# A decoder layer on one core: another order of attention's pools in SBUF

## The chip, the cores and the metric

The kernel runs on one core of a Trainium2 chip. The metric is the device time in microseconds of one execution. A core has five engines that run side by side, each strictly in its own order: TensorE (PE, matrix products; PEld is its loading of weights), VectorE (DVE), ScalarE (ACT), GpSimd (POOL) and SyncE (SP). SP only issues transfers (DMAs); ACT and POOL issue some as well. Engines wait for each other, and for the landing of transfers, by semaphores. SBUF is the working memory on the chip, PSUM the small memory in which TensorE leaves its products, HBM the large memory outside.

## The reference

The input x has 16 sequences of 112 rows of 1024 numbers, 1792 rows in all; ctx has 375 rows for each sequence.

```python
x = _layernorm(x + _L0_attn_ref(x, w_gate, w_up, w_down), axis=-1)      # "x1" in this text
x = _layernorm(x + _L0_xattn_ref(x, ctx, ctx, Wq, Wk, Wv, Wo), axis=-1)
x = _layernorm(x + _L0_ffn_ref(x, qweight, qscale, qzeros), axis=-1)
```

The first step, in spite of its name, is a gated MLP: silu(x w_gate^T), with the half of each row that is smallest in magnitude set to zero, times x w_up^T, times w_down^T. The second is attention of x1 over ctx:

```python
q = (query @ Wq).reshape(b, sq, NUM_HEADS, HEAD_DIM).transpose(0, 2, 1, 3)   # 32 heads of 32
k = (key @ Wk).reshape(b, sk, NUM_KV_HEADS, HEAD_DIM).transpose(0, 2, 1, 3)  # 8, each repeated 4 times
v = (value @ Wv).reshape(b, sk, NUM_KV_HEADS, HEAD_DIM).transpose(0, 2, 1, 3)
probs = jax.nn.softmax(jnp.einsum('bhqd,bhkd->bhqk', q, k) * scale, axis=-1)
out = jnp.einsum('bhqk,bhkd->bhqd', probs, v)
return out.transpose(0, 2, 1, 3).reshape(b, sq, DIM) @ Wo
```

The third is a product with a weight matrix that is stored as 4-bit numbers with scales and zeros.

## The kernel before

The work is done in stages. First come the gates, with the search for each row's median, the up projection, and the keys and values of attention, which are stored to HBM as k_d and v_d. Then comes the down projection in several passes (class Down). Its last pass, `last_pass`, goes over seven pairs of row tiles of 128 rows. For each tile it adds up the products in a tile y (L853 loads the rows of x into it, L859, L874, L875 and L882 add to it), takes the layer norm in place (L72 to L87) and has POOL store it to HBM as 128 rows of x1, `x1_d` (L863). The names in a trace leave numbers out, so this store reads `x_d<-y`. The last of the fourteen stores is the last thing that the MLP does. Beside it, the last pass unpacks the 4-bit weights (L912 to L921) and loads the weights of the query projection, wq_sb. Queries are made for two sequences at a time, from x1 as it is read back from HBM: `fetch` loads 112 rows (xr, L939), `rows` transposes them on TensorE (L950) and ACT copies them out (L951), and `chunk` makes one of eight blocks of 128 query columns (L958, L962). Of the first pair of sequences the first block is made before attention begins.

Then `attention_and_ffn` runs. Its loop goes over 128 units n. A unit is a sequence b, a half c of the key heads (0 or 1) and a number r of four, so four units in a row share one tile of keys, kT_b_c. A unit makes the scores of four heads (L1025), their maxima on DVE (L1031), and their exponentials on ACT into one of three slots of the tile probs (L1033). One unit later the exponentials are divided by their sums (L1041 on DVE, L1042 on POOL), two units later DVE transposes them in blocks of 32 by 32 into a tile named squares (L1053). After every second unit sixteen DMAs move the blocks of the two units to their places in a tile named weights (L1067): eleven are issued by SP, five by POOL. Some units later TensorE multiplies these with the values (L1080), and when a row tile is complete it is projected with wo_sb (L1117) and taken through the last two layer norms (class Tail). Between a unit's scores and those of the next, TensorE makes a chunk of queries or a piece of a projection; two chunks follow unit 0.

Before the loop SP gets, in this order, the keys kT_0_0 (L1004), the two value tiles of sequence 0 (L1008), and wo_sb, the whole matrix Wo of 4 MB, in sixteen DMAs of 256 KB (L1246). The next keys, kT_0_1, which unit 4 is the first to use, are asked for in unit 1, so they come behind wo_sb in SP's order. The first DVE instruction of attention is the memset of the padding of probs (L999).

The order of instructions on each engine is the order in which the program is written (`as_written`). What a framework adds are addresses and semaphores. SBUF is given out by pools. On the left side they are stacked: a pool that is opened later stands at a higher address. When a pool is opened on space that earlier tiles had, its first instructions wait until every earlier instruction on that space is done, and for a DMA that reads or writes there until it has landed. In `attention_and_ffn` five such pools are opened: const (wo_sb), ld (keys, values, rows of x1), work (probs, squares, weights, results), small (sums, maxima, statistics), and the pools in PSUM. The last pass keeps its y tiles on the right side, in a pool that is closed when attention begins.

DMAs that SP and ACT issue carry one of eight semaphores each in turn; a DMA waits until the earlier one with its semaphore has landed. The DMAs that POOL issues have eight of their own.

The bytes of a partition at which these tiles stand, from the built program:

| tile | before |
|---|---|
| parts of the down weights (wd), in use to the end of the last pass | 17312 to 62368 |
| blocks h of the last pass | 62368 to 84896 |
| sums c11, u, v | 84896 to 127904 |
| statistics of the last pass | 132320 to 132548 |
| y, four buffers | 132576 to 148960 |
| wo_sb | 17312 to 50080 |
| keys, values, rows of x1 (ld) | 50080 to 68448 |
| probs, squares, weights and the rest of work | 68448 to 152416 |
| sums, maxima and statistics (small) | 152416 to 153124 |

Of the kernel before, what the change touches and what calls it, by code (L numbers as in the profile page):

```python
# [10 lines left out]
F32 = mybir.dt.float32  # L11
# [11 lines left out]
P = 128  # L23
B, S, D = 16, 112, 1024
NT = B * S
TT = NT // P
KC = D // P
# [937 lines left out]
def attention_and_ffn(nc, tc, ident, ident_b, negh, x1_d, k_d, v_d, queries, wf_sb, wo, out):  # L965
# [14 lines left out]


    with ExitStack() as ctx:
        const = ctx.enter_context(tc.tile_pool(name="a_const", bufs=1))
        wo_sb = const.tile([P, KC, D], F32, tag="wo", name="wo_sb")

        ld = ctx.enter_context(tc.tile_pool(name="a_ld", bufs=2))
        work = ctx.enter_context(tc.tile_pool(name="a_work", bufs=2))
        small = ctx.enter_context(tc.tile_pool(name="a_small", bufs=3))
        ps = ctx.enter_context(tc.tile_pool(name="ps", bufs=3, space=PSUM))
        ps_s = ctx.enter_context(tc.tile_pool(name="ps_s", bufs=1, space=PSUM))  # L990
        ps_o = ctx.enter_context(tc.tile_pool(name="ps_o", bufs=1, space=PSUM))
# [371 lines left out]
def kernel(  # L1363
# [38 lines left out]
    with as_written(nc, tc):  # L1402
        with ExitStack() as psum:
# [30 lines left out]
            for mc in range(EARLY):  # L1434
                queries.chunk(0, mc)
        attention_and_ffn(nc, tc, ident, ident_b, negh, x1_d, k_d, v_d, queries, wf_sb, wo, out)


# [46 lines left out]
```

## Time and profile before

| what | us |
|---|---|
| median of three runs | 2598.56 (2598.23 to 2599.01) |
| the profiled execution | 2598.46 |
| its span, from its first to its last instruction | 2596.7 |
| TensorE busy in the span | 2517.4 (97%) |
| DVE, ACT, POOL busy | 1719.4, 1390.3, 1205.1 |
| mean granted clock of TensorE | 0.987 |
| last store of x1 issued by POOL | 1844.40 |
| wo_sb: first and last of its sixteen loads issued by SP | 1839.1, 1863.2 |
| first product that reads wo_sb | 1961.1 |

The span holds everything that the profile shows; some 1.8 us of the execution lie around it. The MLP takes the first 1840 us, attention with the third step the rest. TensorE is busy nearly all the time in both, so the places to look at are those where it is not, and what ended its idle time there. A line of a timeline gives start, length, engine, line, operation, tiles and count, and in brackets the engine's idle time before it with what ended it. A line of the chain of waits gives start, length, and the engine and line (or the transfer) that the end of the program goes back to at that time. For a DMA the issue is on the queue of its engine (SPq, POOLq, ACTq), and the landing is a time of its own.

### The profile page before, as it was taken

The page shows a single profiled execution, that of the slowest core. Times are in us where ns is not written, and L with a number is a line of the kernel's source. Part 1 is how long each engine was busy: PE and PEld are TensorE (multiplying, and loading weights), DVE is VectorE, ACT ScalarE, POOL GpSimd, SP SyncE. Part 2 cuts the span into 40 slices and gives each one's busy share as a digit, 9 for nine tenths or more (in the row PEclk, how much of TensorE's full clock was granted, in tenths as well). Part 3 has the DMA queues.
Part 4 walks back from the last instruction along what each step waited for, and adds up shares of the span by engine and source line. Part 5 has one row for each costly group of instructions (what it writes and reads, how often), then busy time and mean ns, then how long its engine had stood idle before and what let it go on. Part 6 is the DMA issues. An engine that isn't in the chain of part 4 may idle for free. (4 is left out here: it accounts for less than half of the span.)

```text
span 2596.7 us, 34788 instructions
## 1 busy us (share of the span) xinstructions
PE 2517.4 (97%) x10500; PEld 1526.5 (59%) x10514; DVE 1719.4 (66%) x3634; ACT 1390.3 (54%) x2470; POOL 1205.1 (46%) x1143
## 2 busy tenths in 40 slices
PE   9999999999999999999988999999889999999996
PEld 4444444466666666777764444444566666666763
DVE  0378778878988887677730343247577777777773
ACT  0487787778767877888830000000255565555652
POOL 1113443255557545444250000024387888878883
PEclk9999999999999999999999999999889999999998
DMA  6322322276768668998657223157587778787763
GB/s 243 132 72 83 109 107 73 99 273 237 228 228 281 229 229 275 299 291 290 224 172 251 87 87 109 55 189 232 147 205 186 204 191 199 192 200 197 196 175 95
DMA packets 283609, 478.65 MB, mean 184 GB/s; under 512 B 37856, under 2 KB 208224, under 8 KB 279328
## 3 DMA queue, kind: packets, MB, share of 16 engines
q1 hardware_dynamic: 241184, 374.06, 46.9%
q0 software_dynamic: 27008, 75.76, 9.4%
q10 hardware_dynamic: 15232, 26.62, 3.3%
q8 instruction: 85, 1.39, 0.2%
q14 instruction: 100, 0.82, 0.1%
HBM read 272.12 MB, written 103.50 MB: 145 GB/s over the span
## 5 line engine op out<-in xcount | busy, mean ns | idle before, releaser
L468 ACT ACTIVATE ja<-a,cand 128x1824 int8<-128x1824 f32 x434 | 787.9, 1815 | 195.2 <-DVE cand L480 187.3
L471 DVE TENSOR_SCALAR_CACHE_REDUCE jv<-a,cand 128x928 uint8<-128x928 f32 x434 | 509.6, 1174 | 42.6 <-ACT a L455 35.7
L190 PE MATMUL pg<-wg_sb,xT 128*128 128x456 f32 (+1 forms) x1344 | 519.2, 550 | 2.7 <-DMA wg_sb<-in_wg_dram 2.7
L190 PEld LDWEIGHTS pg<-wg_sb,xT 128*128 128x128 f32 x1344 | 255.8, 191 | 265.6 <-issue 258.7
L1033 ACT ACTIVATE probs<-sc,nmax 128x375 f32<-128x375 f32 x512 | 286.3, 572 | 229.7 <-DVE nmax L1031 213.0
L1042 POOL TENSOR_TENSOR probs<-probs,sums 128x1500 f32<-128x1500 f32 x128 | 344.2, 2689 | 131.8 <-DVE sums L1041 112.8
L1031 DVE TENSOR_REDUCE nmax<-sc 128x2 f32<-128x750 f32 x256 | 228.4, 931 | 128.4 <-PE sc L1025 128.2
L729 PE MATMUL m<-wd,h 128*128 128x512 f32 (+1 forms) x616 | 267.1, 596 | 6.1 <-DMA h<-hT_d 6.1
L297 PE MATMUL pu<-u,xe 128*128 128x344 f32 x896 | 264.1, 453 | 2.3 <-DVE u L317 1.8
L1053 DVE STREAM_TRANSPOSE squares<-probs 128x1536 f32<-128x1536 f32 x128 | 224.0, 1750 | 20.3 <-DMA weights<-squares 10.4
L297 PEld LDWEIGHTS pu<-u,xe 128*128 128x128 f32 x896 | 170.0, 190 | 92.4 <-DVE u L317 2.9
L201 POOL DMA_DIRECT2D s_d<-s x84 | 45.9, 546 | 360.7 <-DVE s L200 297.3
L958 PE MATMUL bank<-x1T,wq_sb 128*128 128x224 f32 x1008 | 210.4, 363 | 0.0
L958 PEld LDWEIGHTS bank<-x1T,wq_sb 128*128 128x128 f32 x1008 | 188.3, 192 | 34.5 <-issue 31.3
L729 PEld LDWEIGHTS m<-wd,h 128*128 128x128 f32 (+1 forms) x616 | 117.5, 191 | 153.8 <-issue 152.3
L297 PE MATMUL pu<-u,xl 128*128 128x344 f32 x672 | 199.6, 453 | 2.5 <-DVE c L330 1.4
L1117 PE MATMUL bank<-wo_sb,aT 128*128 128x256 f32 x832 | 194.6, 388 | 0.0
L951 ACT COPY x1T<-pq 128x448 f32<-128x448 f32 x4 | 1.9, 535 | 349.1 <-DMA sc<-in_qs_dram 331.8
L1117 PEld LDWEIGHTS bank<-wo_sb,aT 128*128 128x128 f32 x832 | 155.1, 191 | 45.9 <-issue 23.3
L1067 POOL DMA_DIRECT2D weights<-squares x320 | 177.7, 561 | 6.9 <-PE po L1080 2.4
L375 PE MATMUL pk<-wv_sb,ctx 128*128 128x256 f32 (+1 forms) x768 | 173.3, 379 | 0.0
L421 POOL TENSOR_TENSOR hs<-hs,hm 128x512 f32<-128x512 f32 (+1 forms) x84 | 96.7, 1159 | 160.8 <-DMA hm<-m_d 151.5
(152 smaller groups left out, 3372.6 us busy)
## 6 DMA issues: line engine op xcount, KB each, us to landing
weights<-squares SPq DMA_DIRECT2D x704, 96.0 KB, 3.4
h<-hT_d SPq DMA_DIRECT2D x56, 640.0 KB, 4.6
weights<-squares POOLq DMA_DIRECT2D x320, 96.0 KB, 3.6
ctx<-in_ctxT_dram SPq DMA_DIRECT2D x16, 1500.0 KB, 8.8
a<-s_d SPq DMA_DIRECT2D x14, 1376.0 KB, 8.5
us<-s_d SPq DMA_DIRECT2D x112, 172.0 KB, 3.7
u_d<-c SPq DMA_DIRECT2D x84, 172.0 KB, 3.2
xe<-in_xT_dram SPq DMA_DIRECT2D x28, 512.0 KB, 5.5
```

Of the source, the lines that this page charges most:

```text
L190: nc.tensor.matmul(pg[:, :w], xts[t][:, kc, :], wg_sb[:, kc, ds(off, w)], start=(kc == 0), stop=(kc == KC - 1),)
L297: nc.tensor.matmul(m, a[i][:, b, ts(n, P)], k[:, n, :], start=(n == 0), stop=(n == KH - 1))
L468: nc.scalar.activation(ja, a[:, NV:], AF.Sign, bias=cand, scale=-1.0, accum_out=st["sgn"])
L471: nc.vector.tensor_scalar(jv, a[:, :NV], cand, -(TOPK - 1 - NA / 2), ALU.is_lt, ALU.add, accum_out=st["nlt"])
L729: self.nc.tensor.matmul(bank, a[:r, k, :], b(k)[:r], start=(k == 0), stop=(k == HK - 1),)
L958: nc.tensor.matmul(pq[:, :GT], self.wq_sb[:, kc, ts(mc, P)], self.x1T[g][:, kc, :], start=(kc == 0), stop=(kc == KC - 1),)
L1031: nc.vector.tensor_reduce(nmax[h], sc[h][:, :, :SK], AX.X, ALU.max, negate=True)
L1033: nc.scalar.activation(pr[:, i, :SK], sc[i // 2][:, i % 2, :SK], AF.Exp, bias=nmax[i // 2][:, i % 2 : i % 2 + 1], accum_out=sums[:, i : i ...
L1042: nc.gpsimd.tensor_tensor(pr, pr, sums.unsqueeze(2).to_broadcast([P, 4, SK]), ALU.mult)
L1053: nc.vector.transpose(sq[:, :, n % 2].rearrange("p k (i f) -> p k i f", f=Q), probs[:, n % 3].rearrange("p i (k f) -> p k i f", f=Q),)
L1067: queue.dma_start(wt[ts(m, Q), :, j], by_part[ts(j, Q), :, m])
L1117: nc.tensor.matmul(pp[:, :256], aT[:, h, r, :], wo_sb[:, h * REP + r, ts(i, 256)], start=(h == 0 and r == 0), stop=(h == 1 and r == REP - 1),)
```

## The change

Two lines go from the top of `attention_and_ffn`'s list of pools to a place behind its pools on the left side.

```diff
     with ExitStack() as ctx:
-        const = ctx.enter_context(tc.tile_pool(name="a_const", bufs=1))
-        wo_sb = const.tile([P, KC, D], F32, tag="wo", name="wo_sb")
 
         ld = ctx.enter_context(tc.tile_pool(name="a_ld", bufs=2))
         work = ctx.enter_context(tc.tile_pool(name="a_work", bufs=2))
         small = ctx.enter_context(tc.tile_pool(name="a_small", bufs=3))
+        const = ctx.enter_context(tc.tile_pool(name="a_const", bufs=1))
+        wo_sb = const.tile([P, KC, D], F32, tag="wo", name="wo_sb")
         ps = ctx.enter_context(tc.tile_pool(name="ps", bufs=3, space=PSUM))
```

The addresses that follow from it, with what stood there in the last pass:

| tile | after | stands where |
|---|---|---|
| keys, values, rows of x1 (ld) | 17312 to 35680 | wd was |
| probs | 35680 to 54112 | wd was |
| squares, weights and the rest of work | 54112 to 119648 | wd, h, c11, u and part of v were |
| sums, maxima and statistics (small) | 119648 to 120384 | v was |
| wo_sb | 120384 to 153152 | the rest of v, the statistics, y, and tiles of the unpacking were |

The two built programs have the same instructions in the same order on every engine; what differs in them are addresses and the semaphores that some instructions wait for. In the program of before, the memset (L999) waits for the landing of the last four stores of x1, and the first of the sixteen loads of wo_sb waits for none of them. In the changed program the memset waits for nothing, and the first load of wo_sb waits for these four stores and for DVE's last layer norm.

## The prediction

> **What bounds the kernel now.** I read the busy shares first, then the stretches around the one place that the change touches, then the waits, the chain and the queues there.
>
> ```profile
> PE 2517.4 (97%) x10500; PEld 1526.5 (59%) x10514; DVE 1719.4 (66%) x3634; ACT 1390.3 (54%) x2470; POOL 1205.1 (46%) x1143
> ...
> 1843.00:1860.00 17.00, 6.52 (x36) 6.13 (x38) 2.65 (x4) 4.10 (x11) 0.85 (x2) 0.74 0.82 200
> 1860.00:1886.00 26.00, 26.00 (x160) 19.86 (x152) 17.40 (x21) 14.60 (x48) 17.92 (x14) 0.91 0.60 139
> ```
>
> The columns of a stretch are its length, then PE, weight loads, DVE, ACT and POOL busy, granted clock, DMA share and GB/s. TensorE is full nearly everywhere; where attention begins it works 6.52 of 17 us. So what is worth anything here is TensorE time between the last product of the MLP and attention's steady run. Who makes it wait:
>
> ```profile
> 1842.64 6.32 PE L958 MATMUL bank<-x1T,wq_sb 128*128 128x224 f32 x32
> 1859.44 1.63 PE L1025 MATMUL sc<-kT,qT 32*128 32x375 f32 x8 [10.48 <-ACT qT L962]
> ...
> 1843.29 0.81 DVE L87 TENSOR_SCALAR y<-y,ln_mv,ln_rstd 128x1024 f32<-128x1024 f32 x1 [0.69 <-POOL ln_rstd L82]
> 1854.47 0.15 DVE L999 MEMSET probs<- 128x108 f32 x1 [10.36 <-DMA x_d<-y]
> ```
>
> TensorE's 10.48 is DVE's 10.36 passed on: the memset of probs (L999) stands until the last rows of x1 have landed, and behind it in DVE's order stand the maxima of unit 0 (L1031), then ACT's exponentials, then the freed banks that unit 1's scores want. The chain shows the same stretch and what follows:
>
> ```profile
> 1844.40 9.89 DMA x_d<-y
> ...
> 1859.44 1.63 PE sc L1025 x8
> 1861.07 5.12 PE bank L958 x16
> 1866.19 0.84 PE sc L1025 x8
> 1867.03 3.22 PE bank L958 x16
> 1870.26 1.06 PE sc L1025 x8
> 1871.32 3.22 PE bank L958 x16
> 1874.54 0.90 PE sc L1025 x8
> ```
>
> After the gap the same work is slow: 1.63 against 0.84 for the scores of a unit, 5.12 against 3.22 for a chunk of queries, 2.69 us together (the granted clock of the stretch from 1860 is 0.91). The piece at 1874.54 is unit 4, the first to use the second key tile, kT_0_1. That tile is loaded by SP, which works in order:
>
> ```profile
> 1837.47 1.60 SPq L1008 DMA_DIRECT2D v<-v_d  x2
> 1839.11 24.71 SPq L1246 DMA_DIRECT2D wo_sb<-in_wo_dram  x16
> 1863.87 0.58 SPq L1004 DMA_DIRECT2D kT<-k_d  x1
> 1874.73 7.12 SPq L1067 DMA_DIRECT2D weights<-squares  x11
> ...
> SPq L1246 <- DMA xr<-x_d: 12.0, 1, 12.0
> ```
>
> The 24.71 us hold a stall of 12.0: eleven of the sixteen loads go out by 1848.1, the twelfth at 1860.7, since it shares a semaphore with the fetch of xr (L939), which ACT issues only at 1856.85, behind its own wait for DVE.
>
> **The change part by part.** No instruction is added, removed or moved: the instruction lists of the two built programs have the same rows in the same order on PE, DVE, ACT and SP, and on POOL but for which copies carry a wait. Only addresses move, and with them waits.
>
> (1) Wait taken away. The memset, the exponential table load and the first weights copy lose their waits for the stores of x1. The memset waits for nothing then. DVE is free at 1843.29 + 0.81 = 1844.10, so the memset goes 10.37 us earlier, unit 0's maxima too (its scores are done at 1841.80 + 0.91 = 1842.71), and unit 1's scores at 1859.44 - 10.36 = 1849.08. TensorE's two query chunks end at 1842.64 + 6.32 = 1848.96, so they cover all but 0.1 us, the gap is gone, and with it the slow 2.69. From unit 1 the warm steps are 0.84 + 3.23 (from 1866.19 to 1870.26, 4.07) and 4.28 (to 1874.54); I take 4.10 + 4.07 + 4.28 = 12.45. TensorE stands before unit 4 at 1861.5 instead of 1874.54: 13.0 us early. DVE and ACT keep step, having done units 2 and 3 at that pace.
>
> (2) Wait added. The first load of wo_sb now waits for those stores, on SP, and behind it stand fifteen more loads, kT_0_1, and the eleven weights copies of units 0 and 1. When does kT_0_1 land?
> - The last store is issued at 1844.40. It took 9.89 because the loads of wo_sb were in the queues; the two before it, at 1827.77 and 1836.30, took 3.0 and 3.3. With 3.3 it lands at 1847.7 (ends 3.0 and 4.0, the latter its longest time beside other loads: -0.3, +0.7).
> - The stall of 12.0 is over: xr is issued 10.3 earlier, 1846.5, and lands 3.9 later, before the twelfth load needs it.
> - wo_sb: the load issued at 1860.71 into empty queues took 3.98, the next landed 1.69 after it, the next three 1.28, 1.30 and 1.30 apart (256 KB each). In the earlier burst the first took 5.2 and nine landings were 1.29 apart. So 1847.75 + 3.98 + 1.69 + 14 x 1.29 = 1871.5 for the sixteenth. Low end, by the mean of all ten intervals of the first burst, 1.21: -1.7; high end +1.2 for a first load of 5.2.
> - kT_0_1 was issued 0.64 after the last load of wo_sb and landed 0.24 after it, 6.63 in all, though a key tile alone takes 3.1 (the one at 1837.08). So it lands behind all of wo_sb: 1871.7.
>
> TensorE waits for it from 1861.5 to 1871.7, 10.2 us, with nothing in its order to cover it: queries and scores are queued strictly. A gap as long as the old one leaves it slow for the same two pieces: 2.69 again (ends 0 and 6.8, half of the 13.65 us for which the clock record at this place shows a half).
>
> (3) The queue behind. The weights copies of units 0 and 1 follow on SP once their semaphores come round, the last at about 1874 and landed by 1877; the product that reads them (L1080) comes after unit 6's scores, in before 1884.50 - 1874.54 = 9.96 after unit 4 started, so now past 1881: at least 4 us of cover. Without it each us late would be paid. wo_sb itself is read first at 1961.1, 89 us after landing. xr comes earlier, for transposes at 1882.79 in before.
>
> (4) Traffic beside wo_sb. Five copies by POOL (480 KB) and xr (448 KB) now run while wo_sb comes in. Bounds: nothing, since beside the x1 store the landings of wo_sb stayed 1.29 apart; or their bytes at wo_sb's own 256 KB per 1.29, 928 / 256 x 1.29 = 4.7 us. The row for a transfer beside wo_sb is the former, so I take 0 and keep 4.7.
>
> The Trainium skill, page "DMA: Bandwidth & Descriptors", section "Queues, rings and completion order", speaks against the change here: each DMA engine takes turns, packet by packet, between the queues that have work, so POOL's copies and xr would push the loads back. By it the 4.7 would count and the sum would be 4.6 slower. The same page, section "Where 436 GB/s comes from", puts the HBM limit of a core near 358 GB/s, 0.73 us per load; by it (an estimate) wo_sb would be in by 1863.6 and the sum about 11 us faster. The landings 1.29 apart contradict that rate for these loads, and the measurement decides.
>
> **Sum.** -13.0 + 10.2 + 2.69 = -0.1 us: unit 4 has lost what unit 1 gained. Against the span of 2596.7 that is 2596.6. The profiled run took 2598.46, 1.8 over its span, and the median of three is 2598.56, so it stands for them; I forecast 2598.5. Its own range, with the ends (-0.3 -1.7 -2.7 and +0.7 +1.2 +4.7), is 2594 to 2605.
>
> **The rivals.**
> A, faster: kT_0_1 does not sit behind all of wo_sb, or wo_sb runs faster without the store between. Issued when the ninth load has landed (1847.75 + 3.98 + 1.69 + 7 x 1.29 = 1862.5) and taking 3.1, it lands at 1865.6; TensorE waits 4.1, slow for 0 to 2.69. -13.0 + 4.1 + 1.3 = -7.6: 2591.0; with no wait at all, -13.0: 2585.6. For it: 404 GB/s moved in the best slice near 1851. Against it: 6.63 for kT_0_1 where nothing but wo_sb was ahead.
> B, slower: the copies by POOL and xr hold the loads up by the 4.7 of part 4, so kT_0_1 lands at 1876.4: 2603.2. It costs from the moment that kT_0_1 lands after 1871.8, and passes 0.2% when it lands after 1877. For it: copies of 96 KB took 2.3 alone and up to 6.2 in company around 1890. Against it: the unchanged landings beside the store.
> C: the change does not do what it says, and the memset still waits: 2598.6. Only the trace can show a semaphore that comes late, but the built program gives the memset none.
>
> **How the numbers follow.** Forecast 0.66, A 0.18, B 0.14, C 0.02. About 0.2% (5.2 us) is what a measurement of this kernel can tell from no change. Faster by more: A, and a little of the forecast's lower edge, 0.20. Slower by more: half of B, and edges, 0.12. Within: 0.68. The range reaches down to A's middle and up past B: 2591.5 to 2604.
>
> **What would show it.** Part 1: the memset beside L87 with no idle time, unit 1's scores near 1849 at 0.84, no gap there. Part 2: SP's wo_sb starting near 1847.7, the store of 1844.40 landing in some 3 us, the loads in one run with no stall of 12, kT_0_1 issued about 1862.5 and landing near 1871.7, and a gap of some 10 us on TensorE before unit 4, with 1.63 and 5.12 after it. Part 3: no wait of the products at L1080 near 1884. I am wrong if that gap is under 5 us (A), if it ends after 1877 (B), or if the stretch from 1886 to 1947, where TensorE idled 1.1 and 5.6 us in before, changes by several us for another reason.

## The result and the profile after

The changed kernel took 2607.24 us, the median of 13 runs (2600.26 to 2615.7), beside 2598.98 for the kernel before (13 runs, 2596.91 to 2608.78). The ratio is 1.0025, 95% interval 1.0015 to 1.0035: slower by some 6.5 us (3.9 to 9.1), where no change was forecast. The profiled execution took 2607.94 with a span of 2606.2, 9.5 longer than the span before. The direction was that of rival B.

First the busy line of the page and two stretches, with the same columns as those shown of the kernel before:

```profile
PE 2521.2 (97%) x10500; PEld 1528.8 (59%) x10514; DVE 1719.0 (66%) x3634; ACT 1390.8 (53%) x2470; POOL 1204.3 (46%) x1143
...
1843.00:1860.00 17.00, 16.55 (x98) 13.48 (x98) 8.87 (x15) 9.86 (x30) 6.20 (x4) 1.00 0.61 148
1860.00:1886.00 26.00, 10.53 (x44) 8.49 (x48) 7.03 (x8) 5.10 (x18) 8.41 (x8) 0.67 0.86 179
```

The hole has moved from one stretch into the next: 6.52 of 17 us before has become 16.55, and 26.00 of 26 has become 10.53. TensorE's timeline shows its new edges:

```profile
1844.41 6.32 PE L958 MATMUL bank<-x1T,wq_sb 128*128 128x224 f32 x32
1850.66 0.91 PE L1025 MATMUL sc<-kT,qT 32*128 32x375 f32 x8
...
1859.86 3.29 PE L958 MATMUL bank<-x1T,wq_sb 128*128 128x224 f32 x16
1878.62 1.75 PE L1025 MATMUL sc<-kT,qT 32*128 32x375 f32 x8 [15.47 <-DMA kT<-k_d]
1880.30 5.50 PE L958 MATMUL bank<-x1T,wq_sb 128*128 128x224 f32 x16
1885.73 0.91 PE L1025 MATMUL sc<-kT,qT 32*128 32x375 f32 x8
```

Unit 1 follows the query chunks with no idle time, as part 1 had it. Then TensorE stands 15.47 us before unit 4, waiting for kT_0_1, and the next two pieces are slow: 1.75 and 5.50 instead of 0.91 and 3.29, 3.05 together. On DVE the memset follows the layer norm at once:

```profile
1844.62 0.81 DVE L87 TENSOR_SCALAR y<-y,ln_mv,ln_rstd 128x1024 f32<-128x1024 f32 x1 [0.69 <-POOL ln_rstd L82]
1845.40 0.15 DVE L999 MEMSET probs<- 128x108 f32 x1
```

SP's queue, what it waited for, and the two instructions of ACT that decide when xr is fetched:

```profile
1849.00 17.15 SPq L1246 DMA_DIRECT2D wo_sb<-in_wo_dram  x16
1866.94 0.33 SPq L1004 DMA_DIRECT2D kT<-k_d  x1
1868.30 13.86 SPq L1067 DMA_DIRECT2D weights<-squares  x11
...
SPq L1246 <- DMA x_d<-y: 9.1, 1, 9.1
```

```profile
1850.77 0.36 ACT L962 ACTIVATE qT<-bank 128x224 f32<-128x224 f32 x1 [0.48 <-PE bank L958]
1850.85 0.32 ACTq L939 DMA_DIRECT2D xr<-x_d  x1
```

The stall of 12.0 in SP's loads is gone, but kT_0_1, issued at 1866.94, lands only at 1878.49. The chain of waits has nothing between them:

```profile
1855.01 11.91 DMA wo_sb<-in_wo_dram
1866.94 11.55 DMA kT<-k_d
1878.49 0.14 issue
1878.62 1.75 PE sc L1025 x8
```

It stood behind the loads of wo_sb, and the landings show that these were late:

| transfer | issued | landed | behind the landing before it |
|---|---|---|---|
| last store of x1 | 1845.73 | 1848.67 | |
| wo_sb, loads 1 and 2 | 1849.00, 1849.71 | 1853.20, 1854.54 | 1.34 |
| wo_sb, loads 3 and 4 | 1850.36, 1850.99 | 1858.40, 1860.64 | 3.86, 2.24 |
| xr, 448 KB, by ACT | 1850.85 | 1860.32 | |
| wo_sb, loads 5 to 13 | 1851.62 to 1861.97 | 1861.96 to 1872.06 | 1.05 to 1.34 |
| POOL's five copies, 480 KB | 1864.54 to 1866.79 | 1873.58 to 1877.91 | |
| wo_sb, loads 14 to 16 | 1863.26 to 1865.59 | 1873.81 to 1877.66 | 1.75, 2.00, 1.85 |
| kT_0_1 | 1866.94 | 1878.49 | 0.83 |

Against 1.29 a load, the loads that ran beside xr are 3.86 + 2.24 - 2 x 1.29 = 3.5 us late, and those that ran beside POOL's copies 5.60 - 3 x 1.29 = 1.7.

One caution for all that follows. The MLP before attention is the same code in every kernel here, and yet unit 0's scores start between 1838.87 and 1845.98 in the fifteen profiled executions. So the table counts from unit 0: the start of a unit's scores behind unit 0's in the same trace, less the same in the kernel before (negative is ahead). The last column is the ratio of the times of many runs, which decides.

| kernel | unit 1 | 3 | 4 | 5 | 7 | 9 | 16 | 20 | 127 | ratio, 95% |
|---|---|---|---|---|---|---|---|---|---|---|
| changed | -10.55 | -12.94 | +2.38 | +5.36 | +5.14 | +6.47 | +6.47 | +7.31 | +7.52 | 1.0025 [1.0015, 1.0035] |
| keys first | -10.55 | -12.94 | -13.16 | -12.93 | +1.02 | +2.40 | +2.41 | +3.02 | +2.82 | 1.0005 [0.9995, 1.0016] |
| wo_sb spread | -10.55 | -12.94 | -13.15 | -12.91 | -13.13 | -6.64 | -6.08 | +2.99 | +6.60 | 1.0014 [1.0001, 1.0027] |
| old pools, spread | -6.56 | -6.67 | -6.66 | -6.66 | -6.66 | +0.48 | +1.66 | +6.19 | +6.43 | 1.0034 [1.0022, 1.0046] |
| xr late | -10.55 | -12.94 | -2.03 | +0.98 | +0.76 | +2.10 | +2.12 | +2.91 | +3.17 | 1.0002 [0.9990, 1.0014] |
| copies on SP | -9.58 | -11.97 | +1.09 | +3.52 | +3.30 | +4.76 | +4.78 | +5.07 | +8.52 | 1.0024 [1.0009, 1.0039] |
| both of these | -10.45 | -12.84 | -2.09 | +0.98 | +1.28 | +3.89 | +5.09 | +5.92 | +9.77 | 1.0016 [0.9999, 1.0033] |
| 96 transposes | -10.49 | -12.88 | +2.25 | +4.96 | +4.75 | +5.98 | +6.00 | +6.47 | +7.46 | 1.0032 [1.0020, 1.0044] |
| 140 transposes | -10.55 | -12.94 | +2.12 | +2.06 | +2.13 | +3.08 | +3.08 | +3.68 | +6.56 | one run |
| 8 + 8 loads | -10.55 | -12.93 | -13.15 | -12.93 | -9.06 | -9.40 | -9.39 | -8.71 | -6.61 | 0.9982 [0.9972, 0.9991] |
| 4 + 12 loads | -10.55 | -12.93 | -13.15 | -12.93 | -10.44 | -7.92 | -3.32 | +3.69 | +0.55 | 1.0015 [1.0004, 1.0026] |
| 8 + 8 on ACT | -10.14 | -12.53 | -12.75 | -12.52 | -8.90 | -9.86 | -9.44 | -7.19 | -6.88 | 0.9977 [0.9966, 0.9988] |
| 11 + 5 on ACT | -10.55 | -12.94 | -13.16 | -12.93 | -4.01 | -6.17 | -4.58 | +0.52 | +0.39 | 1.0002 [0.9991, 1.0013] |
| old pools, 8 + 8 on ACT | -0.57 | -0.39 | -0.39 | -0.40 | +5.19 | +8.03 | +8.41 | +10.48 | +13.95 | 1.0036 [1.0022, 1.0049] |

The changed kernel's 9.5 us of span are then: 1.77 before unit 0, -12.94 up to unit 3, +15.32 from there to unit 4, +2.98 in the slow pieces behind it, 1.95 in smaller losses from there to unit 20, and 0.4 behind that. Of the smaller losses 0.70 can be named: unit 8's scores stood 0.49 and 0.21 us for ACT's exponentials (L1033), which they did not in the kernel before.

### The profile page after: what moved, and what is told of

Same layout as the page of the kernel before. It is cut to its first block, busy times and chain, and to the rows that moved or that the text cites. A ratio compares the mean times of both kernels' runs of the same rounds, so it can differ in the third digit from the quotient of the medians.

```text
span 2606.2 us, 34781 instructions
## 1 busy us (share of the span) xinstructions
PE 2521.2 (97%) x10500; PEld 1528.8 (59%) x10514; DVE 1719.0 (66%) x3634; ACT 1390.8 (53%) x2470; POOL 1204.3 (46%) x1143
## 5 line engine op out<-in xcount | busy, mean ns | idle before, releaser
L1033 ACT ACTIVATE probs<-sc,nmax 128x375 f32<-128x375 f32 x512 | 286.3, 572 | 243.3 <-DVE nmax L1031 225.0
L1067 POOL DMA_DIRECT2D weights<-squares x320 | 177.7, 561 | 7.1 <-PE po L1080 2.4
```

Of the source, the lines that this page charges most:

```text
L1033: nc.scalar.activation(pr[:, i, :SK], sc[i // 2][:, i % 2, :SK], AF.Exp, bias=nmax[i // 2][:, i % 2 : i % 2 + 1], accum_out=sums[:, i : i ...
L1067: queue.dma_start(wt[ts(m, Q), :, j], by_part[ts(j, Q), :, m])
```

## The experiments

All but two start from the changed kernel. The edits leave what is computed as it is.

**What lies beside wo_sb's loads.** Three kernels take away the transfers that ran beside the loads: xr, POOL's copies, and both.

```diff
-            if fetched == turned < B:
+            if fetched == turned < B and (fetched > GB or n >= 4):
```

> The changed kernel, with the fetch of xr for the third sequence (448 KB, ACT's queue) moved from behind unit 0 to behind unit 4, so that it does not run beside wo_sb. In the changed kernel the third and fourth loads of wo_sb landed 3.86 and 2.24 us after the ones before, 3.5 us more than two steps of 1.29. Theory: that is xr's share; without it kT_0_1 lands 3.5 us earlier against the first scores than in the changed kernel, where it landed 34.9 after them: 31.4, and the time is 3.5 lower, about 2604. Rival: the rate of wo_sb does not depend on its company, and kT_0_1 lands 34 to 35 after them.

The time was 2603.44 us beside 2600.47. All sixteen loads landed 1.2 to 1.3 apart, and kT_0_1 landed 30.5 us after unit 0's scores began, in the changed kernel 34.9. Next, the copies:

```diff
-                queue = nc.gpsimd if i >= 16 - SOFT else nc.sync
+                queue = nc.gpsimd if i >= 16 - SOFT and n > 1 else nc.sync
```

> The changed kernel, with all sixteen weights copies of units 0 and 1 on SP (five of them are on POOL in the changed kernel, and ran beside the last loads of wo_sb, whose landings then came 1.75, 2.00 and 1.85 apart instead of 1.29). Theory: kT_0_1 lands 2 us earlier against the first scores (32.9 instead of 34.9), and the landings stay 1.3 apart to the end; the time falls by 2 at the most, less what five more copies on SP cost later. Rival: landings still slow down at the end, and 34.9.

2606.42 beside 2600.47; the loads' last landings stay about 1.3 apart, and kT_0_1 landed 33.6 after unit 0, 1.3 earlier than in the changed kernel. With both edits:

> The changed kernel with both moves, xr late and the copies of units 0 and 1 on SP. Theory: the two add up, kT_0_1 lands 5.5 to 6 us earlier than in the changed kernel against the first scores (29 to 29.5 instead of 34.9), which is the time that the forecast had for it, and the whole kernel comes to about 2601, 6 below the changed one and 0 to 3 over the kernel before. Rival: the two overlap, or something else fills the queues, and kT_0_1 lands at 31 or later.

2605.43 beside 2600.47, and kT_0_1 again 30.5 after unit 0. The edge before unit 4, first with xr late, then with both:

```profile
1876.62 1.75 PE L1025 MATMUL sc<-kT,qT 32*128 32x375 f32 x8 [11.05 <-DMA kT<-k_d]
1878.30 5.53 PE L958 MATMUL bank<-x1T,wq_sb 128*128 128x224 f32 x16
```

```profile
1875.60 1.88 PE L1025 MATMUL sc<-kT,qT 32*128 32x375 f32 x8 [10.91 <-DMA kT<-k_d]
1877.41 5.45 PE L958 MATMUL bank<-x1T,wq_sb 128*128 128x224 f32 x16
```

15.47 becomes 11.05 and 10.91, where 10.2 had been forecast, and unit 5 stands at +0.98, near the forecast's -0.1. The traffic beside the loads is what the forecast lacked, and xr is nearly all of it: with xr alone out of the way the ratio falls from 1.0025 to 1.0002, and taking the copies away as well gains nothing more at unit 4.

With xr late the copies still ran (issued 1866.96 to 1869.20), and the loads that landed while they were under way kept their 1.25 to 1.32. The 1.3 us of the kernel with copies on SP are not the copies' alone either: there the loads began 6.72 us behind unit 0 instead of 5.43, and xr, issued between the first two loads, made the second 1.6 us late (2.89 less 1.29) instead of 3.5 for two. So no run gives a price of the copies by themselves. Both edits together were a miss in time: about 2601 was expected. Sixteen copies on SP cost later: 1.43 of waiting for weights just ahead of unit 7, and +5.92 at unit 20.

**The place of kT_0_1 in SP's order.** The keys are asked for ahead of wo_sb, and the loop's own request for them is left out.

```diff
         load_values(0, 1)
+        load_keys(0, 1)
...
-            if n % 4 == 1 and n // 4 + 1 < 2 * B:
+            if n % 4 == 1 and 0 < n // 4 and n // 4 + 1 < 2 * B:
```

> The changed kernel, with one move: kT_0_1 is issued before the loads of wo_sb. Theory: SP's queue is late for the weights copies of units 0 and 1 too, since their semaphores come round only when the last loads of wo_sb have landed (in the changed kernel the last copy landed at 1883.8). TensorE then runs units 4 to 6 without a gap and stands at the first product with the values (L1080) from about 1873 to 1883, slow afterwards: about as the kernel before, 2599 (2596 to 2602), with the wait moved once more. Rival: kT_0_1 alone was late; then no wait of over 2 us at L1080 and 2586 to 2589.

2601.07 beside 2599.78. The gap before unit 4 is gone and all 13 us are kept, until the first product with weights:

```profile
1886.67 2.79 PE L1080 MATMUL po<-weights,v 128*32 128x256 f32 x24 [13.79 <-DMA weights<-squares]
...
SPq L1067 <- DMA xr<-x_d: 8.7, 1, 8.7
```

The next thing in SP's queue is late in its stead, as the theory had it. Part of that 13.79 is a turn of semaphores: SP stood 8.7 us at a copy (L1067) for the landing of a fetch of xr, which had the semaphore that the copy needed.

**wo_sb in single loads.** The sixteen loads are taken out of the block and issued one behind each unit from 0 to 15, with the new pools and with the old ones.

```diff
-        for i in range(4):
-            for r in range(REP):
-                nc.sync.dma_start(by_rep[ts(i, HD), r], by_head[ts(r, HD), i])
+        wo_parts = deque((i, r) for i in range(4) for r in range(REP))
+        def load_wo():
+            i, r = wo_parts.popleft()
+            nc.sync.dma_start(by_rep[ts(i, HD), r], by_head[ts(r, HD), i])
...
+            if n >= 0 and wo_parts:
+                load_wo()
             lights(n)
```

> The changed kernel, but the sixteen loads of wo_sb are issued one behind each of the units 0 to 15 instead of all before the loop. Theory: the changed kernel loses because kT_0_1 stands behind 4 MB of wo_sb on SP (15.5 us of gap before unit 4, then some 3 us of slow clock). With that gone, no gap at unit 1 and none over 1 us at unit 4, unit 4 about 13 us earlier than in the kernel before: 2599 - 13 = 2586 (2584 to 2590). Rival 1: the new addresses of the working tiles make attention slower as a whole; then the gap goes but the time stays at 2597 or more. Rival 2: the pieces of wo_sb between the weights copies hold SP up later on: a new wait at L1080 of several us, 2590 to 2597.

2604.38 beside 2599.78: rival 2's waits, at a higher price than it had. TensorE is 13.1 ahead through unit 7 and then loses it all. SP's waits and one of TensorE's:

```profile
SPq L1067 <- DMA xr<-x_d: 13.7, 3, 5.9
```

```profile
1893.45 2.79 PE L1080 MATMUL po<-weights,v 128*32 128x256 f32 x24 [4.15 <-DMA weights<-squares]
```

> The kernel before (its order of pools), with the loads of wo_sb issued one behind each of the units 0 to 15. The memset of probs still waits for the stores of x1. Theory: the store took 9.9 us only because the loads of wo_sb were in the queues, so it lands in about 3.0 and the memset waits 3.3 instead of 10.4: 7 us saved, and up to 2.7 of slow clock: 2599 - 7 to 2599 - 10 = 2589 to 2592, that is 3 to 6 us over the changed order of pools with the same spread loads. Rival: the store is slow by itself, and the memset waits 9 to 10 us as before: 2597 or more.

2609.17 beside 2599.78: a miss. With the loads out of its way the store lands in time for unit 1 to come 6.56 earlier even with the old pools, but the same waits follow. In the kernel before, the DMA engines were 62 to 72% busy in the four slices of 10 us from 1900 to 1940; an estimate from that: two loads in the 9.84 us that a pair of units takes there, 2 x 1.29 = 2.6 or 26%, take nearly all that was left.

**The slow pieces behind the gap.** Transposes of the identity into a bank that nobody reads stand before unit 4's scores, 96 in one kernel and 140 in the other (WARM in the edit). (Line numbers are higher by 1 up to there.)

```diff
+            if n == 4:
+                idle = bank()
+                for _ in range(WARM):
+                    nc.tensor.transpose(idle[:, :P], ident, ident)
             sums[n] = scores(n)
```

> The changed kernel, with 96 transposes of the identity on TensorE (results unused) between the chunk after unit 3 and the scores of unit 4, where it waits for kT_0_1. Theory: the gap makes the next two pieces slow by 3.0 us (7.11 us from unit 4 to unit 5 instead of 4.1). With the gap filled, unit 4 starts at the same time but takes 4.1 to unit 5: 3 us less than the changed kernel, about 2604. Rival: the slowness is not due to the gap, and unit 4 still takes 7 us: 2607, or more if the transposes run into the arrival of the keys.

> The changed kernel with 140 instead of 96 idle transposes before unit 4's scores: 140 x 0.111 = 15.5 us, which fills the gap that 96 left (4.81). Theory (idle time of TensorE is what slows the clock afterwards): unit 4's four scores take 0.9 instead of 1.75 and the query chunk behind them 3.3 instead of 5.2 to 5.5; unit 5 starts 2 to 3 us nearer to the kernel before's than with 96. Rival (transposes don't count as work for the clock): 1.75 and 5.2 again, with a gap below 1 us.

The timeline with 96, then with 140:

```profile
1862.11 10.64 PE L1308 MATMUL bank<-ident 128*128 128x128 f32 x96
1877.56 1.75 PE L1026 MATMUL sc<-kT,qT 32*128 32x375 f32 x8 [4.81 <-DMA kT<-k_d]
```

```profile
1858.29 15.45 PE L1308 MATMUL bank<-ident 128*128 128x128 f32 x140
1873.67 0.91 PE L1026 MATMUL sc<-kT,qT 32*128 32x375 f32 x8
1874.51 3.29 PE L959 MATMUL bank<-x1T,wq_sb 128*128 128x224 f32 x16
```

The 96 ended 4.81 us too early and changed nothing (2608.73 beside 2599.78); 140 reach the landing of the keys, and the pieces take 0.91 and 3.29. Unit 4 starts at the same place (+2.25, +2.12), unit 5 at +2.06 instead of +4.96. So the slow pieces come from TensorE's idle time and cost 2.9 us; 4.81 of idle time bring them as well as 15.47 do.

The traces' record of the granted clock shows why the length matters little. It stands at a half from 1867.74 to 1884.80 in the changed kernel, from 1851.22 to 1864.87 in the kernel before and from 1876.37 to 1883.19 with 96 transposes. Only 6.18, 5.43 and 5.63 us of this fall on work behind the gap, and half of each, 3.1, 2.7 and 2.8, is about what the slow pieces cost (2.98, 2.69, 2.71). Work that produces nothing keeps the clock up (with 140 the granted clock from 1855 to 1885 is 1.00).

The page "TensorE: Matmul & The Clock Gate" of the Trainium skill, section "HAM oscillation — how this bites in real kernels", asks for no gaps above some 3.4 us; the 4.81 agrees with it. But shorter gaps were not safe here. Behind 2.49 us in one kernel below (eight and eight loads) the clock was at a half for 3.41 us, and the next transposes (L950) took 1.64 instead of 0.93. Behind 2.41 us in another (eight and eight on ACT) it was so for 3.41 us too, from 2.5 us later on: the transposes took 0.99, and the product L1080 behind them 2.79 instead of 1.50. In the kernel before, a half of 6.83 us begins at 1888.77, where no idle time in the 29 us ahead was over 0.91. So the length of one idle time does not tell by itself when the clock falls. The 140 were run once, so this rests on one trace and not on the time.

**A place for wo_sb.** The keys go first, xr waits for unit 4, and the loads are split: some before the loop, the others behind single units, on SP's queue or on ACT's. Of the edits only the last is new; this is eight and eight on ACT.

```diff
+        for _ in range(8):
+            load_wo(nc.sync)
...
+            if wo_parts and n in range(4, 20, 2):
+                load_wo(nc.scalar)
             lights(n)
```

> The changed kernel with kT_0_1 fetched ahead of wo_sb, the second group's xr not before unit 4, eight wo_sb loads before the loop, and the other eight one behind every second unit from unit 4 to unit 18. Theory (the sixteen loads in one piece are 20.6 us of the DMA engines, 16 x 1.29, and what stands behind them is late; one load in each 8.3 us, where the engines were 62 to 73% busy, fits): the weights copies of units 0 and 1 come some 10 us earlier than where the keys alone went first, so there the wait of 13.79 at L1080 shrinks below 4; TensorE is 9 to 13 us ahead of the kernel before at unit 8, still 7 to 13 at unit 16, and the time is 2586 to 2593, ratio 0.995 to 0.998. Rival (any place costs the engines the same 20.6 us, which come back as waits before unit 20): ahead by 13 at unit 7, by less than 4 at unit 20, time 2597 to 2603, ratio 0.999 to 1.002.

> As the run with eight and eight, but four loads before the loop and twelve one behind each unit from 4 to 15. Theory: two loads in each 8.3 us are as dense as where all sixteen were spread, so the waits for weights copies and for xr come back in units 8 to 16; ahead by 13 at unit 7, by 0 to 5 at unit 16, time 2596 to 2602. Rival (what cost there was only that the loads began at unit 0, before the copies' first use): ahead by 10 or more at unit 16, time 2586 to 2592.

> As the run with eight and eight, but the later eight are issued by ScalarE's queue instead of SP's. Theory (the DMA engines are what is shared): within 1.5 us of that run at unit 16 and in time. Rival (SP's queue order is what holds the copies up): 2 us or more better at unit 16, as the copies no longer stand behind loads. ScalarE pays about 0.3 us for each of eight issues, 2.4 in all, most of it beside TensorE.

Eight and eight took 2594.78 us beside 2599.8 (ratio 0.9982) and on ACT 2592.53 (0.9977): both are faster than the kernel before, by 4.7 us (2.3 to 7.3) and 6.0 (3.1 to 8.8), their intervals overlapping. That is a little short of the theory's 2586 to 2593 for eight and eight. Four and twelve took 2602.9. With eight on ACT the 13 us shrink in small waits:

```profile
1871.67 0.99 PE L950 MATMUL bank<-ident,xr 112*128 112x112 f32 x8 [2.41 <-DMA xr<-x_d]
...
1874.33 2.79 PE L1080 MATMUL po<-weights,v 128*32 128x256 f32 x24 [0.84 <-DMA weights<-squares]
...
1926.97 2.79 PE L1080 MATMUL po<-weights,v 128*32 128x256 f32 x24 [3.65 <-DMA weights<-squares]
```

The wait of 13.79 for the weights is down to 0.84. One load in each pair of units fits; two, as in the kernel with twelve, lose 7.1 us from unit 7 to unit 16 and 7.0 more by unit 20, where the product waits 6.85 us for weights; with eight on SP the longest such wait between these units is 2.06. How full the engines are does not tell the two apart: from 1900 to 1950 they were 92% busy with twelve and 97% with eight. Whether the loads stand in SP's queue or in ACT's made 0.05 us of difference at unit 16.

**Is it the pools at all, and is there more room?** The first of the two last kernels has these same moves (eight and eight on ACT) on the old pools. The second has the new pools, eleven loads ahead and five on ACT behind units 8, 10, 12, 14 and 15, since with eight the engines stood idle between the landing of the last load at 1859.65 and the next transfer, issued at 1861.25.

> The kernel before, with its old order of the pools, and the same three moves as the run with eight loads before the loop and eight on ScalarE's queue: keys first, xr not before unit 4, and the eight later loads behind every second unit. Theory (the order of the pools is worth something once the loads no longer come in one piece): the eight first loads, issued from about 1839, still stand in the engines beside the last x1 store, which lands near 1852 instead of 1854, so unit 1 comes only 2 to 4 us earlier than before instead of 10.1, the clock is slow behind that gap, and the time is 2595 to 2600, ratio 0.998 to 1.000, 3 to 7 us behind the same placing with the new pools. Rival (the order of the pools is worth nothing, the placing is all): 2592 to 2594, ratio 0.9970 to 0.998.

> The changed kernel with keys first, xr not before unit 4, eleven wo_sb loads before the loop and five on ScalarE's queue behind units 8, 10, 12, 14 and 15. With eight, the eighth landed at 1859.65 and the next transfer was issued at 1861.25, so the DMA engines stood idle for some 3.5 us, the room of three loads. Theory (what is lost behind unit 5 is the DMA engines' room): the waits for xr at units 6 and 7 (2.4 and 0.7) and for the weights copies at unit 8 fall as no load stands among them; ahead by 11 to 13 at unit 8 and by 8 to 11 at unit 20, time 2589 to 2592, ratio 0.996 to 0.9975. Rival (the three loads run into the copies of units 0 and 1): ahead by 9 or less at unit 8, and the time as with eight or worse, 2592 to 2597.

On the old pools the same moves took 2609.94 us beside 2601.23, a ratio of 1.0036 where the new pools gave 0.9977, further back than expected. Its memset and unit 1:

```profile
1856.31 0.15 DVE L999 MEMSET probs<- 128x108 f32 x1 [8.94 <-DMA x_d<-y]
```

```profile
1861.29 1.63 PE L1025 MATMUL sc<-kT,qT 32*128 32x375 f32 x8 [9.91 <-ACT qT L962]
```

Eight loads before it are enough to hold the store up for 8.47 us (2.95 alone), so unit 1 gains 0.57 instead of 10.14. The order of the pools is worth 12.1 us at unit 5, and this placing needs it. From unit 5 to unit 7 the old pools lose 5.6 more, with a wait of 3.63 for xr and 6.83 us of half clock behind it; their losses after that were not taken apart. With eleven loads ahead the time was 2601.19 beside 2601.23, the rival's side:

```profile
1884.23 2.79 PE L1080 MATMUL po<-weights,v 128*32 128x256 f32 x24 [7.71 <-DMA weights<-squares]
```

```profile
SPq L1067 <- DMA xr<-x_d: 3.8, 1, 3.8
```

The trace shows the rival's cause in another form than it was put. The last of the eleven loads landed at 1867.59, after the copies had begun at 1865.86. ACT then issued xr at 1869.91 with a semaphore that SP's seventh copy needed; xr landed at 1874.65, and that copy was issued at 1874.67. The last of SP's eleven copies went out 31.4 us after unit 0, with eight loads ahead 28.1. The idle room was there (the engines were 7% busy from 1859.65 to 1861.25 with eight), but filling it moved the turn of the semaphores.

## Why the prediction was wrong, step by step

**Part 1 held.** The memset without idle time, unit 1's scores behind the chunks, no slow pieces there: 12.94 us ahead at unit 3, where 13.0 was forecast for the stretch before unit 4.

**Part 2 failed in one step.** The store landed in 2.95 (3.3 forecast; its upper end of 4.0 was taken for the longest time of such a store, but three earlier ones had taken 5.09 to 6.89), the first load of wo_sb took 4.20 (3.98), the loads that had nothing beside them 1.29 each, and SP had no stall of 12. What failed is "xr issued 10.3 earlier, 1846.5". Its issue stands in ACT's queue behind the copies of unit 0's two query chunks (L962). Before, these chunks were long done when ACT came there; with the gap gone ACT waits for TensorE's second chunk, until 1850.77. So xr came at 1850.85, between the third and the fourth load, not ahead of them all. No run issues it ahead of them, so what this step cost by itself is not shown.

**Part 4 is where the size was lost: "so I take 0 and keep 4.7".** This term of the sum was mis-sized: it measured 5.2 (3.5 beside xr, 1.7 beside the copies); by undoing it 4.4, all with xr alone. The row that it was taken from, loads 1.29 apart beside the x1 store, is a mean of 1.00 to 1.54, and doesn't speak for the loads: there it was the store that paid, 9.89 instead of 2.95. Here loads 3 and 4, which shared the engines with xr until it landed at 1860.32, paid for it as well as xr. Its 448 KB at the loads' own rate would be 2.3 us, and they cost 3.5. Other traces, where the same fetch was issued behind the first, third or fourth load, reckoned in the same way give 1.6 (copies on SP, 140 transposes), 2.4 (keys first) and 4.0 (96 transposes), so the size of 3.5 is that of one execution. The taking of turns between queues that the prediction cited against the change, from the Trainium skill's page "DMA: Bandwidth & Descriptors" (section "Queues, rings and completion order"), had the right sign, and its 4.6 slower was nearer than the forecast.

**The sum as measured** to unit 5 is -12.94 + 15.32 + 2.98 = +5.36, for -13.0 + 10.2 + 2.69. The slow clock behind the gap was right in its place and nearly in size. Its upper end of 6.8 was half of the whole 13.65, most of which fell on the gap itself, and the sum's own range had left that end out. kT_0_1 landed at 1878.49; by unit 0's clock, which is 1.77 later in this trace, the forecast's 1871.7 is 1873.5 and rival B's 1876.4 is 1878.2. B was the right case with the right mechanism, though nearly all of it was xr's and little the copies', and got 0.14.

**Part 3 held for the changed kernel**: no wait at L1080 in units 6 to 8. But the last of SP's copies went out at 1881.55, 1879.8 by the clock of before and not about 1874, so its cover was lent by the gap. With the gap taken away the product waits 13.79.

**Rival A** needed a kT_0_1 that doesn't stand behind wo_sb. Moving it there brought back only what was then lost at the weights, so its 2585.6 was out of reach of that one edit. Rival C fell with the memset.

What stays open: but for 0.70 the 2.2 us between units 7 and 20 of the changed kernel were not taken apart, nor the scatter of 7.1 us before unit 0.

## What to carry to other kernels

A wait that is taken off one engine and laid on a queue of transfers moves the whole queue, and with it what stands behind: price everything that must pass through the DMA engines in that stretch, and ask when each of these transfers will be issued in the new order, not in the old one. When two streams run side by side, look at which of them paid; that one came through unharmed says nothing of the other, nor of the reverse. If a block of transfers only moves a wait from one reader to the next, as here with keys, weights and rows, the remedy that paid here was to split it and place its parts. How much a step bears had to be tried (eight and eight gained, four and twelve and eleven and five did not), and it paid only with the change that seemed to lose.

## What the runs showed of the hardware beside that

- A transfer issued into a block of others takes far longer than alone: xr 9.47 us beside the loads, 3.85 in the kernel before, where no load was under way; a store of x1 8.47 behind eight loads, 2.95 without them.
- Transfers of two engines that share semaphores in turn stop each other: copies on SP waited 3.8, 5.9 and 8.7 us for a fetch issued by ACT, though the data have nothing to do with each other.
- 140 transposes that nobody reads, 0.11 us each, kept TensorE's clock at 1.00 over a wait, and 4.81 us without work brought it to a half for 6.83 us.
